# Changing when an attention kernel issues its loads, normalizations and PSUM copies

## The chip, the cores and the metric

The kernel runs on one core of a Trainium2 chip. The metric is device time in microseconds (us) of one execution. A core has five engines that run their own instruction streams: PE (TensorE, matrix products), ACT (ScalarE), DVE (VectorE), POOL (GpSimd) and SP (SyncE, which here only issues DMAs). An engine runs its instructions in the order in which they were put in its stream; a wait for a semaphore holds everything behind it on that engine. All data are float32.

## The reference

Two layers of attention over x of shape (4, 256, 64, 64), four images of 256 channels with 64 x 64 tokens each.

```python
# layer 0: 8 heads of 32 channels, 4096 queries, 1024 keys
n = GroupNorm32(x)
q = conv1x1(n, Wq); k = conv2x2_stride2(n, Wk); v = conv2x2_stride2(n, Wv)
a = softmax((q @ k + q @ (rel_h + rel_w)) * 32**-0.5)
x = x + a @ v
# layer 1: four areas of 1024 tokens per image, attention inside an area
n = GroupNorm32(x)
q, k, v = split(conv1x1(n, w_qkv) + b_qkv)          # 8 heads of 32
o = softmax(q @ k * 32**-0.5) @ v
x = x + conv1x1(o + depthwise7x7(v) + b_pe, w_proj) + b_proj
```

GroupNorm has no weights: each of 32 groups (8 channels by 4096 tokens) is brought to mean 0 and variance 1.

## The kernel before

**Blocks, units, steps, phases.** The work is cut into eight blocks: A0 to A3 and then B0 to B3 (`BLOCKS`), where A is layer 0 of an image and B is layer 1 of it. A block has 16 units (`UNITS`): eight chunks of 512 queries by two groups of four heads. A unit has eight steps (`NKT`): one tile of 128 keys each. So there are 128 units and 1024 steps. The main loop at the end of `direct_path` runs 683 phases (`PHASES`); a phase computes one full step and half a step (256 of the 512 queries), so 1.5 steps. A unit is thus 5 1/3 phases.

**What a phase does.** `scores` (L423) puts four heads' scores of its one and a half steps into three double PSUM banks; three exps on ACT (L465 twice, L476 for the half step) turn them into p in SBUF. Meanwhile PE multiplies the p of the phase before with v (`weighted`, L490), which adds up in a PSUM bank `av` for the whole unit. DVE adds up the same p into `acc` (`add_up`, L500), since a softmax needs the sum over all keys. Between these PE takes side work: one or two parts of a queue.

**End of a unit.** When a unit's last products with v are done, `evict` copies av to SBUF (`av_sb`, L1122, on ACT). There are two small PSUM banks in turn (`banks`): one holds av, the other serves side products (`ps_side`). When DVE's sums are complete, `divisors` (L509) adds them over partitions on PE, and `divide` copies the result (`den_sb`, L523, on ACT). Then it spreads the divisors over partitions by way of DRAM, all issued by POOL: `rows` (L524), `few` (L525), and later, after the reciprocal on DVE (L531), `recs` (L533) and four loads of `rb` (L535). The last step multiplies av_sb with rb into `att` (L538, DVE).

**What orders the rest.** Nothing reorders the program: each engine's stream is the order in which this Python code calls it. Four lists decide the order.

- `at(g, j, f)`: f is called at the end of the phase that reaches step j of unit g. Loads, means and variances, and hand-timed additions hang here. SP issues DMAs in the order of these calls.
- `task` and `task_at`: side work in parts (`side`), with a due time and a condition `ready`. `choose` takes the one with the earliest due time that is ready. `pressure` and `supply` reckon how many parts a phase must take; `credit` carries the rest over. Products of k, q, v, the value products, the projection and the convolution are such tasks, and each part is mostly one "side product" of 512 columns.
- `quick` (filled by `soon`): one entry at a time runs in a phase that has no other side work begun, no unit boundary and no division due. The group means and group variances of `plan_norm` (L347 to L364) go this way.
- `later`: normalizations on ACT (L387), run by `norm_next` at the end of a phase if the phase has room by `busy`, and if the phase number has reached `start`. If a task needs one that hasn't run, `settle` runs it at once. In the same way `normalize` runs the quick queue empty if its scale doesn't exist yet.

In the text a "call phase" is the phase of the loop in whose turn an instruction is put in the streams. Its DMA may issue later, if SP is held or behind.

**Normalizations.** `plan_norm` aggregates statistics at step j, and calls `means` at j + 1 and `variances` at j + 3. `variances` has one small product on PE, ACT's copy `gvar`, then three POOL operations: pow (L359), a product (L363) and a sign (L364), which give `norm_A` or `norm_B`. The normalizations read them: of `taps` (A's input for k and v, from `xa` loads), `hq` (A's chunk of queries, loaded by `fetch`, normalized 4 phases or more later), `h` (B's area, loaded by `load`, normalized at a planned step with no minimum), and `hv` (B's chunk for values, loaded at L950 by `plan_values`, 3 steps ahead of `when`, normalized 4 phases or more later).

**The convolution.** `plan_values` makes v for the whole image as `vout` and stores it to DRAM twice: to `vala` for the attention (L975) and, per column parity, to `vals` for the convolution (L983). The 7x7 depthwise convolution runs on PE as products with band matrices. A `share` is the data for 8 channels: a `band` of matrices (L1024) and rows of vals in `rows` or `share` tiles, by four DMAs. The first shares of an image are forced by `plan_conv`, `room` of them (2 for image 0, 3 for the others, which also use the space of weights no longer needed): each of these calls tests that less than `room` are loaded, then calls `load_share(True)`. `convolve` calls `load_share(False)` after each share that it has used. It stores its result as `cout` (L1055) to `conv`. `load_rest` loads it back as `cv` (L801, 16 row DMAs per chunk), `add_conv` (L813) adds it to att, and `project` (L828) ends with the output chunk. `load_v` (L739) loads `vc`, the attention's v, from vala.

**Buffers.** Chunk tiles (`xs`, `xa`, `hq`, `xc`, `hv`, `xm`, `cv`) share one pool of 6 buffers. `h` and the taps have 3, `vc` 4, `band` 2, `rows` 2, `vout` 2, `av_sb` 2, `rb` 1. A load into a buffer that is still in use waits on SP, and all later DMAs of SP with it.

Of the kernel before, what the change touches and what calls it, by code (L numbers as in the profile page):

```python
# [60 lines left out]
def direct_path(  # L61
# [124 lines left out]
    def at(g, j, f):  # L186
        g, j = g + int(j // NKT), int(j % NKT)
        plan.setdefault((g, j), []).append(f)
# [83 lines left out]
    def begun():  # L272
        return bool(side) and side[0][2]
# [57 lines left out]
    def plan_norm(key, g, j):  # L331

        name = f"{key[0]}{key[1]}"
        made = {}

        def aggregate():
            for tag, cols in (("mv", 2), ("gmean", 1), ("dev", 1), ("gvar", 1)):
                shape = [P, CT, cols] if cols > 1 else [P, CT]
                made[tag] = pool.tile(shape, FP, tag=tag, name=f"{tag}_{name}", bufs=2)
            mv = made["mv"]  # L340
            for t in range(CT):
                V.bn_aggr(out=mv[:, t, :], in_=stats[key][:, t].rearrange("p c s -> p (c s)"))

        def means():
            mv, mean, dev = made["mv"], made["gmean"], made["dev"]
            ps = ps_side(f"gm_{name}")[:, :CT]
            T.matmul(ps, lhsT=gmat, rhs=mv[:, :, 0], start=True, stop=True)  # L347
            S.copy(mean, ps)
            V.tensor_sub(dev, mv[:, :, 0], mean)
            V.tensor_mul(dev, dev, dev)  # L350
            V.tensor_add(dev, dev, mv[:, :, 1])

        def variances():
            ps = ps_side(f"gv_{name}")[:, :CT]
            T.matmul(ps, lhsT=gmat, rhs=made["dev"], start=True, stop=True)
            S.activation(made["gvar"], ps, AF.Identity, bias=eps)
            norm = pool.tile([P, 2, CT], FP, tag="norm", name=f"norm_{name}", bufs=8)
            shift, rstd = norm[:, 0, :], norm[:, 1, :]
            G.tensor_tensor(rstd, made["gvar"], neghalf, ALU.pow)  # L359
            if key == ("A", 0):  # L360
                V.scalar_tensor_tensor(shift, made["gmean"], -1.0, rstd, ALU.mult, ALU.mult)
            else:
                G.tensor_tensor(shift, made["gmean"], rstd, ALU.mult)  # L363
                G.tensor_scalar(shift, shift, -1.0, None, ALU.mult)  # L364
            norms[key] = shift, rstd

        def quietly(f, n):
            f()
            if key == ("A", 0):
                keep_busy(n)  # L370

        if key == ("A", 0):
            at(g - 1, 0, lambda: keep_busy(44))
        at(g, j, aggregate)
        at(g, j + 1, lambda: soon(lambda: quietly(means, 4)))
        at(g, j + 3, lambda: soon(lambda: quietly(variances, 10)))

    def normalize(key, dst, src, t, by_vector=False):
        while key not in norms:
# [169 lines left out]
    def plan_a(b, u, prep):  # L549
# [129 lines left out]
        for c in range(NCH):  # L679
            g = u + 2 * c  # L680
            at(g - 3, 4, lambda c=c: fetch(c))
            for t in range(CT):
                at(g - 2, 1 + 2 * t, lambda c=c, t=t: later(
                    ("hq", b, c), lambda: norm_chunk(c, t), fetched["q", c] + 4, True
                ))
            for qd in range(2):
                task_at(NKT * (g - 2) + 4, 2, make_q, c, qd, due=g - 0.3, ready=normed("hq", b, c))
            at(g + 3, 0, lambda c=c: load_residual(c))
            at(g + 4, 1, lambda c=c: add_residual(c))
            at(g + 4, 2, lambda c=c: store_chunk(c))  # L690
# [11 lines left out]

    def plan_b(b, u):
        key = ("B", b)
        hs = {}

        def load(a):
            hs[a] = pool.tile([P, CT, TA], FP, tag="h", name=f"h1_{b}_{a}", bufs=3)
            for half in range(2):
                nc.sync.dma_start(hs[a][:, :, half * CH : (half + 1) * CH], xmid[b][2 * a + half])  # L710
# [59 lines left out]
        for a in range(NAREA):  # L770
            g = u + 4 * a
            at(g - 6, 3, lambda a=a: load(a))
            for t in range(CT):
                at(g - 5, 2 + 3 * t, lambda a=a, t=t: later(("hs", b, a), lambda: norm(a, t), 0, True))
            for n in range(4):
                task_at(
                    NKT * (g - 4) + 1 + 4 * n, 2, make_k, a, n // 2, n % 2, due=g - 0.4, ready=normed("hs", b, a)
                )
            for n in range(4):
                at(g - 3, 1 + 2 * n, lambda a=a, n=n: load_v(a, n))  # L780
                at(g - 2, 1 + 2 * n, lambda a=a, n=n: make_v(a, n))
        for c in range(NCH):
            for qd in range(2):
# [77 lines left out]
        for c in range(NCH):  # L861
            g, j = (u + 2 * c + 4, 1) if b < B - 1 or c < NCH - 2 else (u + 2 * c + 3, 7)
            if b == B - 1 and c == NCH - 1:
                for t in range(CT):
                    at(g - 2, 2 + t, lambda c=c, t=t: load_rest(c, t))
                at(g - 2, 4, lambda c=c: load_residual(c))
                at(g - 1, 1, lambda c=c: add_conv(c, [0]))
                at(g - 1, 3, lambda c=c: project_last(c))
                continue
            for t in range(CT):  # L870
                at(g - 2, 7 + 4 * t, lambda c=c, t=t: load_rest(c, t))
            at(g - 1, 6, lambda c=c: load_residual(c))
            at(g, j, lambda c=c: add_conv(c))
            for to in range(CT):
                task_at(NKT * g + j + 2, 2, project, c, to, due=g + (2.2 if b < B - 1 else 3), lag=0)
# [67 lines left out]
    def plan_values(b, c, start):  # L943
# [44 lines left out]
                stored[b, c] = True  # L988

        when = int(start * NKT)  # L990
        at(0, when - 3, load)
        for t in range(CT):
            at(0, when + 5 + t, lambda t=t: later(("hv", b, c), lambda: norm(t), made["at"] + 4, True))
        for t in range(CT):
            task_at(
                when + 7, 2, values, t, due=start + 4,
# [6 lines left out]
    def load_share(must):  # L1003

        if not shares:
            return
        b, k = shares[0]
        for c in range(NCH):
            if must:
                need(stored, (b, c))  # L1010
            elif (b, c) not in stored:
                return
        shares.popleft()
        row, size = C * XT, TC * XT
        if b and (b * (C // TC) + k) % 3 == 2:
            place = const.tile([P, 2 * CT * 4 * C], FP, tag="wkv", name=f"share_{b}_{k}")
            n = 2 * NY * size
            xs = place[:NP, :n].rearrange("p (h y c x) -> p h y c x", h=2, y=NY, c=TC)
            band = place[:NP, n : n + 2 * TY * TX * TC].rearrange("p (h y m) -> p h y m", h=2, y=TY)
        else:  # L1020
            band = pool.tile([NP, 2, TY, TX * TC], FP, tag="band", name=f"band_{b}_{k}", bufs=2)
            xs = pool.tile([NP, 2, NY, TC, XT], FP, tag="rows", name=f"rows_{b}_{k}", bufs=2)
        loaded[b, k] = band, xs, phase[0]
        nc.sync.dma_start(band, mats[k])  # L1024
        for a in range(4):
            p = NP // 2 * (a % 2)
            nc.sync.dma_start(
                xs[p : p + NP // 2, a // 2].rearrange("p y c x -> p y (c x)")[:, :, : size - 3],
                bass.AP(
                    tensor=vals[b].tensor, offset=vals[b].offset + k * size + a,  # L1030
                    ap=[[row, NP // 2], [TY * TX * row, NY], [1, size - 3]],
                ),
            )
# [121 lines left out]
    while f < PHASES or before or plan or side or quick or norms_left or to_add or to_divide:  # L1155
# [12 lines left out]
        for s, u in before[:cut]:  # L1168
            accumulate(s, u)
        if cut:  # L1170
            evict(before[0][0] // NKT)
            copies[0] += 1
        exps[2]()
        _, rate = pressure()
        parts = done_den = 0
        if due and not begun():
            done_den = 1
            copies[0] += 1
            g = to_divide.popleft()
# [7 lines left out]
        elif quick and not begun() and not cut and f < PHASES:  # L1187
            quick.popleft()()
        else:
            wanted = credit + max(min(supply(), 2.0), min(rate, 2.0))  # L1190
            if rate > 2:
                parts = side_parts(4)
            elif rate > 1.5 or due or f >= PHASES or wanted >= (0.8 if cut else 1.5):
                parts = side_parts(2)
            elif begun() and side[0][0] % 2:
                parts = side_parts(1)
            elif boundary(mine):
                parts = side_parts(2) if wanted >= 0.9 else 0
            elif wanted >= 0.5 and not cut or begun():
                parts = side_parts(1)  # L1200
            credit = max(-0.5, min(wanted - parts, 0.5))
            if cut and not parts and not begun():
                banks.reverse()
        for s, u in before[cut:]:
            accumulate(s, u)
        add_ready()
# [617 lines left out]
```

## Time and profile before

| what | value |
|---|---|
| three runs | 3127.77, 3136.34, 3136.4 us; median 3136.34 |
| the profiled execution | 3135.3 us, span 3133.6 us |
| mean granted TensorE clock | 0.994 |
| PE | 3067.2 us busy, 98% |
| DVE | 2517.6 us, 80% |
| ACT | 2459.1 us, 78% |
| POOL | 485.4 us, 15% |
| instructions | 110020 |
| DMA | 423.71 MB, mean 135 GB/s |
| first exp begins | 71.2 us |
| last exp ends | 3107.5 us |

The span is from the first to the last recorded instruction; the profiled execution's own time is 1.7 us longer. The busy time of PE is modelled at its ends, so it says little about how close the loop is to its limit. The views used below are these. The page's fifth part lists groups of instructions: code line, engine, operation, destination and sources, shape and count, then busy time and mean duration in ns, then the idle time of that engine ahead of the group and what ended most of it. The waits of an engine list the waiting instruction, the producer it waited for, and after it total us, number and longest. The timeline has one line for each instruction or run of like instructions: start in us, duration, engine, code line, operation, tiles, count, and in brackets the wait ahead of it with what ended it. A queue such as SPq stands for the moment an engine issues a DMA. The windows view has one line for a stretch of time: its length, then for PE, PE's weight load, DVE, ACT and POOL the busy time with instruction counts, then the granted TensorE clock (PEclk), the mean busy share of the DMA engines, and GB/s.

### The profile page before, as it was taken

The numbers are of one execution on the slowest core, as the hardware profiler recorded it, in microseconds if no ns is written. First come the engines' busy times: TensorE is split into PE (matmuls) and PEld (weight loads), VectorE is DVE, ScalarE is ACT, GpSimd is POOL, SyncE is SP. The second block draws the span as 40 slices with busy tenths as digits, with TensorE's granted clock in tenths as the row PEclk, the third lists the DMA queues.
The fourth block names the chain that finished last, engine by engine and source line by source line (L and its number), as shares of the span: only waits on it lengthen the run. The fifth ranks groups of instructions, "written<-read, shape, count | busy, mean of one in ns | idle before, by whom it ended". The sixth has DMA issues, their size and how long they took to land. (4 is left out here: it accounts for less than half of the span.)

```text
span 3133.6 us, 110020 instructions
## 1 busy us (share of the span) xinstructions
PE 3067.2 (98%) x47254; PEld 1272.4 (41%) x47254; DVE 2517.6 (80%) x2721; ACT 2459.1 (78%) x2988; POOL 485.4 (15%) x921
## 2 busy tenths in 40 slices
PE   9999999999999999999999999999999999999998
PEld 6444443444344443334344443333444444343332
DVE  3788987788878778767688887777888888888888
ACT  3888887888888888778788787777777777787875
POOL 0111111112121111111112111111111111111111
PEclk9999999999999999999999999999999999999999
DMA  5344443565434566767865667767655555632222
GB/s 187 66 94 114 101 98 73 112 151 140 94 105 114 151 156 167 160 164 194 207 156 133 163 167 167 178 177 180 161 155 144 150 161 147 160 105 71 52 67 67
DMA packets 648323, 423.71 MB, mean 135 GB/s; under 512 B 411772, under 2 KB 556636, under 8 KB 647832
## 3 DMA queue, kind: packets, MB, share of 16 engines
q1 hardware_dynamic: 619384, 380.11, 47.9%
q0 software_dynamic: 28448, 36.48, 4.7%
q8 instruction: 379, 6.21, 0.9%
q14 instruction: 112, 0.92, 0.1%
HBM read 318.32 MB, written 98.09 MB: 133 GB/s over the span
## 5 line engine op out<-in xcount | busy, mean ns | idle before, releaser
L500 DVE TENSOR_TENSOR acc<-acc,p 128x1024 f32<-128x1024 f32 x1790 | 2113.6, 1218 | 436.9 <-PE av L490 190.5
L465 ACT ACTIVATE p<-s 128x1024 f32<-128x1024 f32 x1194 | 1160.0, 1024 | 432.8 <-PE s L423 417.6
L476 ACT ACTIVATE p<-s 128x1024 f32<-128x1024 f32 x598 | 617.9, 1033 | 0.7 <-PE ops L167 0.3
L423 PE MATMUL s<-q,k_A 32*64 32x256 f32 (+1 forms) x10928 | 555.6, 501 | 24.0 <-ACT p L465 21.7
L423 PE MATMUL s<-q,k_B 32*64 32x512 f32 (+1 forms) x10912 | 549.8, 497 | 4.4 <-ACT p L465 2.5
L490 PE MATMUL av<-p,v_A 128*32 128x256 f32 (+1 forms) x4784 | 454.0, 489 | 0.0
L490 PE MATMUL av<-p,v_B 128*32 128x512 f32 (+1 forms) x4776 | 451.3, 487 | 0.0
L423 PEld LDWEIGHTS s<-q,k_A 32*64 32x64 f32 x10928 | 260.4, 131 | 370.5 <-issue 140.7
L423 PEld LDWEIGHTS s<-q,k_B 32*64 32x64 f32 x10912 | 259.0, 130 | 348.5 <-issue 139.2
L535 POOL DMA_DIRECT2D rb<-recs x508 | 252.5, 503 | 548.8 <-DMA recs<-few 463.4
L533 POOL DMA_DIRECT2D recs<-few x127 | 70.1, 552 | 1401.1 <-DVE sums L532 1253.4
L490 PEld LDWEIGHTS av<-p,v_B 128*32 128x32 f32 x4776 | 149.8, 110 | 263.8 <-issue 237.7
L490 PEld LDWEIGHTS av<-p,v_A 128*32 128x32 f32 x4784 | 150.2, 110 | 230.8 <-issue 189.3
L465 ACT ACTIVATE acc<-s 128x1024 f32<-128x1024 f32 x172 | 166.9, 1023 | 86.4 <-PE s L423 86.4
L509 PE MATMUL den<-acc,ones 128*32 128x512 f32 x1024 | 142.7, 604 | 6.9 <-DVE acc L500 4.5
L525 POOL DMA_DIRECT2D few<-rows x127 | 71.4, 562 | 470.0 <-DMA rows<-den_sb 463.7
L167 PE MATMUL vals_ps<-hv,wqkv_sb 128*32 128x512 f32 x1024 | 126.7, 609 | 3.4 <-DVE xm L828 3.2
L167 PE MATMUL ops<-cv,wp_sb 128*32 128x512 f32 x1024 | 125.1, 598 | 4.9 <-DVE cv L813 2.9
L167 PE MATMUL k1ps<-h,wqkv_sb 128*32 128x512 f32 x1024 | 123.8, 598 | 2.6 <-ACT k_B L730 1.9
L167 PE MATMUL q1ps<-h,wqkv_sb 128*32 128x512 f32 x1024 | 124.5, 599 | 1.4 <-DVE xm L828 1.4
L167 PE MATMUL q0ps<-hq,wq_sb 128*32 128x512 f32 x1024 | 123.8, 597 | 1.2 <-ACT q L662 0.7
L167 PE MATMUL k0ps<-taps,wkv 128*32 128x256 f32 x2048 | 123.2, 382 | 0.4 <-ACT taps L387 0.4
(103 smaller groups left out, 2156.2 us busy)
## 6 DMA issues: line engine op xcount, KB each, us to landing
rows<-vals SPq DMA_DIRECT2D x384, 195.9 KB
rb<-recs POOLq DMA_DIRECT2D x508, 64.0 KB, 3.1
share<-vals SPq DMA_DIRECT2D x128, 195.9 KB
vala<-vout SPq DMA_DIRECT2D x128, 144.0 KB
vals<-vout SPq DMA_DIRECT2D x128, 144.0 KB
vc<-vala SPq DMA_DIRECT2D x64, 288.0 KB
band<-mats SPq DMA_DIRECT2D x96, 176.0 KB
hq<-in_x SPq DMA_DIRECT2D x32, 512.0 KB
```

The source lines that it names most:

```text
L167: T.matmul(out[cols, :], lhsT=lhsT[:, cols], rhs=rhs, start=start, stop=stop)
L423: T.matmul(out[n : n + WIDE], lhsT=unit[2]()[rows, unit[0], j * P + n : j * P + n + WIDE], rhs=unit[1]()[rows, cols], start=True, stop=True,)
L465: S.activation(p, (a, b)[n], AF.Exp, scale=SCALE)
L476: S.activation(p, c.rearrange("p b (l n) -> p b l n", l=2), AF.Exp, scale=SCALE)
L490: T.matmul(out, lhsT=v[:, j, unit[0] * P + HD * h : unit[0] * P + HD * h + HD], rhs=rhs, start=(j == 0 and not u), stop=(j == NKT - 1), sk ...
L500: V.tensor_add(to, to, p)
L509: T.matmul(dens[g][HD * h : HD * h + HD, :], lhsT=ones, rhs=p(h), start=(n == 0), stop=(n == len(sets) - 1),)
L525: G.dma_start(few[:, 0, :], rows.rearrange("h (q n) -> (h q) n", n=CH // HD))
L533: G.dma_start(recs.rearrange("h (q n) -> (h q) n", n=CH // HD), few[:, 1, :])
L535: G.dma_start(rb[HD * h : HD * h + HD, :], recs[h : h + 1, :].to_broadcast([HD, CH]))
```

## The change

It has five parts, all of which move calls to other phases; the arithmetic stays the same.

1. `plan_norm`: for all images but A0 (whose g is below 0) `variances` is queued at step j + 6 instead of j + 3.
2. Normalizations need older loads: hq at least 5 phases after its load (before 4), h at least 6 (before 0), hv at least 6 (before 4). To have it so, hv is loaded 5 steps ahead of `when` instead of 3.
3. `load_v` is called six steps sooner: at g - 4, step 3 + 2n, instead of g - 3, step 1 + 2n. `load_rest` is called at g - 2, steps 5 and 8, instead of 7 and 11.
4. `load_share(True)` does nothing if 3 shares (2 for image 0) are already loaded. Before, only the caller tested the number, against the room of its own image, while the share next in line can still belong to the image before.
5. In the loop, a phase that holds the end of a unit (`cut`) is called bare if it will take no side work and no division. In a bare phase `evict`'s copy of av comes behind the third exp on ACT; before, it was always ahead of the third exp. `wanted` is computed ahead of the exp for that, and `credit` is set from it.

```diff
-        at(g, j + 3, lambda: soon(lambda: quietly(variances, 10)))
+        at(g, j + (6 if g >= 0 else 3), lambda: soon(lambda: quietly(variances, 10)))
...
-                    ("hq", b, c), lambda: norm_chunk(c, t), fetched["q", c] + 4, True
+                    ("hq", b, c), lambda: norm_chunk(c, t), fetched["q", c] + 5, True
...
-        hs = {}
+        hs, since = {}, {}
 
         def load(a):
+            since[a] = phase[0]
...
-                at(g - 5, 2 + 3 * t, lambda a=a, t=t: later(("hs", b, a), lambda: norm(a, t), 0, True))
+                at(g - 5, 2 + 3 * t, lambda a=a, t=t: later(("hs", b, a), lambda: norm(a, t), since[a] + 6, True))
...
-                at(g - 3, 1 + 2 * n, lambda a=a, n=n: load_v(a, n))
+                at(g - 4, 3 + 2 * n, lambda a=a, n=n: load_v(a, n))
...
-                at(g - 2, 7 + 4 * t, lambda c=c, t=t: load_rest(c, t))
+                at(g - 2, 5 + 3 * t, lambda c=c, t=t: load_rest(c, t))
...
-        at(0, when - 3, load)
+        at(0, when - 5, load)
         for t in range(CT):
-            at(0, when + 5 + t, lambda t=t: later(("hv", b, c), lambda: norm(t), made["at"] + 4, True))
+            at(0, when + 5 + t, lambda t=t: later(("hv", b, c), lambda: norm(t), made["at"] + 6, True))
...
         b, k = shares[0]
+        if must and len(loaded) >= (3 if b else 2):
+            return
...
         if cut:
-            evict(before[0][0] // NKT)
             copies[0] += 1
-        exps[2]()
         _, rate = pressure()
         parts = done_den = 0
-        if due and not begun():
+        wanted = credit + max(min(supply(), 2.0), min(rate, 2.0))
+        bare = cut and not begun() and not due and f < PHASES and rate <= 1.5 and (wanted < 0.8 or not choose())
+        if cut and not bare:
+            evict(before[0][0] // NKT)
+        exps[2]()
+        if bare:
+            evict(before[0][0] // NKT)
+            banks.reverse()
+            credit = min(wanted, 0.5)
+        elif due and not begun():
...
-            wanted = credit + max(min(supply(), 2.0), min(rate, 2.0))
...
-            if cut and not parts and not begun():
-                banks.reverse()
```

## Prediction

> **What bounds the kernel now.** I read the page first, then the waits of ScalarE, then the timeline around the longest of them.
>
> ```profile
> PE 3067.2 (98%) x47254; PEld 1272.4 (41%) x47254; DVE 2517.6 (80%) x2721; ACT 2459.1 (78%) x2988; POOL 485.4 (15%) x921
> ...
> L465 ACT ACTIVATE p<-s 128x1024 f32<-128x1024 f32 x1194 | 1160.0, 1024 | 432.8 <-PE s L423 417.6
> ```
>
> TensorE (PE) looks full, but the share is no yardstick: its ends are modelled. So I measured the loop's own beat: from the timeline, the distance between the first L465 exp of one phase and of the next. Phases with one side product of 512 columns (four matmuls side by side) have a median of 3.794 us, with two 4.652 us. The difference, 0.858 us, is one such product, so these phases run at TensorE's pace of 2.937 + 0.857 x products; the second line agrees, for an exp that waits waits for PE's scores. Phases without side work take 3.25 us. By the program's order the 683 phases hold 1086 products and 38 have none: 645 x 2.937 + 1086 x 0.857 + 38 x 3.25 = 2948.6 us. First exp 71.2 us, after the last exp 26.1 us: 3045.9 of the span of 3133.6 us. The other 87.7 us are excess over the beat, four fifths of it in some 40 places. Only that can be won.
>
> ```profile
> ACT p L465 <- PE s L423: 417.6, 506, 2.9
> ...
> ACT hv L387 <- DMA hv<-xmid: 10.6, 3, 6.5
> ...
> ACT hq L387 <- DMA hq<-in_x: 7.4, 2, 6.6
> ACT hv L387 <- POOL norm_B L364: 6.1, 1, 6.1
> ```
>
> Columns are total us, times, longest. The first line is the beat. The other three are few and long: a normalization (L387) on ScalarE (ACT) waits for its load or its scale, all exps queue behind it, and PE runs dry. Three such events:
>
> ```profile
> 1346.86 0.39 SPq L1055 DMA_DIRECT2D conv<-cout  x1
> 1361.46 0.30 SPq L1024 DMA_DIRECT2D band<-mats  x1
> ```
>
> ```profile
> 1377.47 0.61 ACT L523 COPY den_sb<-den 128x512 f32<-128x512 f32 x1
> 1384.56 0.81 ACT L387 ACTIVATE hv<-hv,norm_B 128x512 f32<-128x512 f32 x1 [6.48 <-DMA hv<-xmid]
> ```
>
> At 1346.86 SyncE (SP) issued a store, and then nothing for 14.6 us: the next load, a band of convolution matrices, had to wait for its buffer. Everything behind it came late, an hv load too, and ACT stood 6.48 us.
>
> ```profile
> 1502.03 0.39 SPq L108 DMA_DIRECT2D hq<-in_x  x1
> ...
> 1510.43 0.81 ACT L387 ACTIVATE hq<-hq,norm_A 128x512 f32<-128x512 f32 x1 [6.57 <-DMA hq<-in_x]
> ...
> 1513.12 2.90 PE L423 MATMUL s<-q,k_A 32*64 32x256 f32 x28 [5.45 <-ACT p L465]
> ```
>
> Here hq was issued 22.7 us after its phase began (1479.3), and landed 8.4 us later: ACT waited 6.57 us, PE 5.45 us.
>
> ```profile
> 503.06 0.55 POOL L533 DMA_DIRECT2D recs<-few  x1 [11.27 <-DVE sums L532]
> 507.69 1.99 POOL L535 DMA_DIRECT2D rb<-recs  x4 [4.08 <-DMA recs<-few]
> 509.69 0.74 POOL L359 TENSOR_TENSOR norm_B<-gvar_B,neghalf 128x2 f32<-128x2 f32 x1
> ```
>
> The scale of the first hv (pow, L359) stood in GpSimd's (POOL's) queue behind rb, which waited for recs to land. ACT waited 6.13 us, and the phase took 6.76 us over its beat.
>
> ```profile
> 1380.00:1395.00 15.00, 8.82 (x108) 3.06 (x104) 9.00 (x11) 8.24 (x10) 3.12 (x6) 0.77 0.85 209
> ...
> 2200.00:2400.00 200.00, 200.00 (x3128) 82.28 (x3124) 166.18 (x171) 155.41 (x183) 32.56 (x63) 1.00 0.60 155
> ```
>
> In the third number from the end, PEclk, a stall shows a second time: 0.77 of 15 us, so 3.4 us of clock lost, against 1.00 in quiet stretches.
>
> **What the Trainium skill says.** "TensorE: Matmul & The Clock Gate", Part 1: the array falls to half rate after about one idle window of 3.4 us. The trace agrees: its clock records show 0.5 for 6.83 us from 511.4, 1258.9 and 1385.2, for 10.24 us from 1511.5 and for 3.41 us from 1931.3, each after such a stall. So a stall that goes takes up to 3.4 to 5.1 us of clock with it. "DMA: Bandwidth & Descriptors", Anatomy of one DMA: DMA engines do not wait on semaphores; the wait happens on the issuing sequencer before dispatch. The hole at 1346.86 agrees: what waits for a buffer holds all later DMAs of its queue. "Trainium Kernel Development and Optimization", Performance Expectations, calls matmul busy time a bad metric; 98% beside 87.7 us of excess agrees.
>
> **The change part by part**, from the order of both built programs and the durations above. Both hold 1086 products; phases without any go from 38 to 37, -0.3 us. The classes stay; what counts are stalls.
>
> *load_share.* Before, the first forced load for image 1 fetched image 0's share 30 as a third share, though two buffers exist; that is the hole (call phase 286, released by PE in 292). Now the guard returns, and share 30 is asked for in phase 291, when its buffer comes free. With hv loaded two steps (one to two phases) sooner as well, hv of phase 295 is issued some 25 us sooner than it was. What goes: phases 294-295 7.51 us over the beat, 297 1.34 (half clock), 299 and 301 0.91 (vout waiting for stores behind the hole), 305 2.52 (sums late because L958 waited 5.6 us for those stores). Together 12.3. I take 11, range 9 to 12.3. Its price: shares of image 1 are loaded two ahead, no longer three, so some are issued only 6 phases (28 us) before use. Cover is the 15 to 20 us that issue and landing take; if that is gone, PE waits at 317, up to 3 us.
>
> *Older loads.* By call phases, hq was normalized at least 4 phases after its load and is now at least 5, h 4 and now 6, hv 5 and now 6 or more. In phases 310 to 323 SP is never idle for long and lags its phases by 12 to 24 us (stores of vout took 2.5 to 4.4 us to issue); the excess is 1.56 + 2.33 + 9.54 - 0.32 = 13.1. hv in 310 and 318 (waits 1.67 and 2.45) now stands ahead of ten share DMAs and four stores, 7 to 12 us of issue: gone. But hq of 321 has the same place behind the same DMAs. If it still lands at 1510.4, its norm now ends phase 322 instead of 321: phase 324, at 1523.1 before, starts at 1511.2 + 4.65 = 1515.9, so 7.2 is won, or 3.9 if the clock still halves. I take 5, range 4 to 13.
>
> *Group means further apart.* Variances move 2 or 3 phases for images A2, A3, B2 and B3; for B0 and B1 they stay, since a normalization or the queue forces them, and so does the 6.76 at phase 102. Phase 158 (1.16 over) and 73 (0.67) are mended: 1.8. For A2 it costs: variances go from phase 73 to 76, and hq now leaves its place on ACT in 76 to the first taps of A2, which need that scale at once. Before, POOL and ACT did this there:
>
> ```profile
> 393.52 2.00 POOL L535 DMA_DIRECT2D rb<-recs  x4 [2.66 <-DMA recs<-few]
> 395.52 0.61 POOL L524 DMA_DIRECT2D rows<-den_sb  x1
> 398.76 0.58 POOL L525 DMA_DIRECT2D few<-rows  x1 [2.63 <-DMA rows<-den_sb]
> ```
>
> ```profile
> 393.80 0.60 ACT L523 COPY den_sb<-den 128x512 f32<-128x512 f32 x1
> 394.26 0.85 ACT L387 ACTIVATE hq<-hq,norm_A 128x512 f32<-128x512 f32 x1
> ```
>
> POOL's pow now comes behind rb, rows and few, and few waits for rows to land. So pow starts at 399.3; with L363 and L364 (1.96 us from 380.96 on, in phase 73) the scale is there at 401.3. ACT has copied den and gvar by 394.8 and waits 6.5 us; all exps of phase 77 wait behind it, as after 509.69. There 6.13 us of wait cost 6.76 + 1.20 (half clock): 8.0 us. I take 8 lost, range 5 (rows lands as fast as 1.7 us) to 9.
>
> *hv sooner* also asks for a chunk buffer sooner. One request cannot be met: hv 6 of image 1, in phase 254 instead of 256, needs a buffer that PE frees in phase 259.
>
> ```profile
> 1207.14 0.35 SPq L950 DMA_DIRECT2D hv<-xmid  x1
> ```
>
> Before, the ten share loads of phase 256 went out ahead, from 1192.95 to 1199.3. Now they stand behind this load, and go out from 1207.5 to 1214; PE wants them from 1218.5. At 5 to 8 us to land, PE waits 0 to 4. I take 1.5. The stores behind them come 7 us later and still end before 1228.9, when vout is wanted.
>
> *v and convolution results sooner.* 64 loads and 512 small ones are the same, earlier by 4 phases and by 1.3 to 2. DVE waited 1.69 for vc (2144) and 1.11 for cv; 461 and 463 are 2.51 over. Most DVE waits there are for rb (29.6 + 14.3 us), which these don't touch except by sharing queues. I take 2, range 0 (they collide with recs) to 5.
>
> *Copy behind the third exp.* In 9 bare phases av_sb (0.59 us) goes behind the exp that frees the last scores bank. Bare phases are 0.3 to 0.65 over and the one after up to 0.36. ACT's sum is the same, so only PE's earlier start counts: 2, range 0.5 to 4.
>
> Sum: 0.3 + 11 + 5 + 1.8 + 2 + 2 - 8 - 1.5 = 12.6 us. The profiled execution took 3135.3 us (span 3133.6 and 1.7 around it), 1 us under the median of 3136.34: 3122.7, say 3123.
>
> **Rivals.** (1) *The stalls go with their clock losses.* If hq lands under way (SP lagging 5 us less), older loads bring 9, load_share 12.3, DVE 4.5, copy 3, and rows lands fast (5 lost): 0.3 + 12.3 + 9 + 1.8 + 4.5 + 3 - 5 = 25.9, so 3109. For it: all min ages grow. Against: DMA share 0.75 to 0.85 there. (2) *Given back*: load_share 9, older loads 4, variances 0.7, copy 0.5, and 9 + 4 lost: about 3134. For it: SP and the DMA rings, not the age, set when things land around 1450 to 1510. (3) *Slower*: SP standing at hv 6 of image 1. If the share loads behind it take over 12 us to land instead of 8, PE stands over one window at 1219: 4 + 3.4 of clock, and vout at 1229 and 1233 waits 3.5 for its stores: 11 on top of rival 2, 3145. It decides from 4 us of wait on. Against: DMA share 0.61 there. (4) That the change doesn't do what it says is true for B0 and B1 and counted.
>
> **How the numbers follow.** Forecast 0.46 (3115 to 3129), rival 1 0.28, rival 2 0.14, rival 3 0.12. The range 3107 to 3136 leaves out the ends of rivals 1 and 3. About 0.3% (3126.9 to 3145.7) can't be told from no change; faster: 0.36 of the forecast, 0.28, 0.01: 0.65. Slower: 0.07 of rival 3. Same: 0.28.
>
> **What would show it.** No SP hole before band near 1347 and no hv wait at 1384; half-clock records from 1385 and perhaps 1511 gone; a new taps wait for norm_A of 5 to 7 us near 395 to 401, with a new half-clock record; norm_B's wait at 511 kept; an SP hole near 1181 to 1207; ACT's waits for hv and hq under 6 us together. It is wrong if taps don't wait near 401, or if excess grows in 345 to 470 (rb).

## The result and the profile after

The changed kernel takes 3111.24 us (median of four executions, 3109.85 to 3113.68). The kernel before, measured beside it, has a median of 3132.72 us over its four. The ratio is 0.9933, 95% interval 0.9914 to 0.9952, so the change made the kernel faster by 0.5 to 0.9%. The profiled execution took 3110.89 us, with a span of 3108.5 us.

The page's line of busy times and its line of the exps, of the changed kernel (columns as before):

```profile
PE 3059.6 (98%) x47254; PEld 1269.4 (41%) x47254; DVE 2517.8 (81%) x2721; ACT 2459.3 (79%) x2988; POOL 484.9 (16%) x921
...
L465 ACT ACTIVATE p<-s 128x1024 f32<-128x1024 f32 x1194 | 1161.4, 1026 | 428.1 <-PE s L423 416.7
```

Nothing was saved in work: the counts are the same, DVE and ACT are busy for the same time to 0.2 us. PE is busy for 7.6 us less with the same matmuls, which goes with the clock records further down. The exps wait for PE's scores as before (416.7 us for 417.6), so I take the beat as unchanged and look for the gain by place. I used the beat of the prediction again: a phase should take 2.937 us + 0.857 us for each side product, or 3.25 us with none. What a phase takes beyond that is its excess. Summed over stretches of phases, for two profiles of each kernel:

| phases | what lies there | before | before, again | after | after, again |
|---|---|---|---|---|---|
| 66-81 | scale of A2, first taps of A2 | 0.69 | 0.70 | 11.66 | 13.21 |
| 101-109 | scale of B0, first hv | 8.24 | 8.39 | 7.39 | 7.25 |
| 256-267 | hv 6 of image 1 | 1.99 | 1.99 | 3.41 | 3.25 |
| 268-281 | A3's vout and q | 9.33 | 8.77 | 5.95 | 7.47 |
| 282-293 | last shares of image 0 | 1.11 | 1.11 | 4.10 | 5.72 |
| 294-309 | behind the hole at 1346.86 | 12.60 | 10.67 | 1.40 | 1.45 |
| 310-323 | hq 7 of A3 (phase 321) | 13.65 | 12.47 | 2.11 | 2.54 |
| 412-471 | cv, vc, rb of B0 and B1 | 18.27 | 19.96 | 7.64 | 11.17 |
| others | | 21.9 | 21.7 | 15.8 | 15.2 |
| sum | | 87.7 | 85.8 | 59.5 | 67.3 |

Excess fell by 28.2 us in the first pair. The span fell by 25.1, because the first exp came at 74.4 us instead of 71.2 (the last section is on that). In the second pair, excess fell by 18.5 us. The first pair overstates the gain: the profiled execution of the kernel before took 3135.3 us, at the upper end of its executions (3127.77 to 3136.4), and the medians differ by 21.5 us. Stretches that differ between two profiles of one kernel (268 to 293 and 412 to 471 above all) say the least.

ScalarE's waits in the changed kernel (total us, times, longest us):

```profile
ACT taps L387 <- POOL norm_A L364: 6.5, 1, 6.5
...
ACT hv L387 <- POOL norm_B L364: 5.6, 1, 5.6
...
ACT hq L387 <- DMA hq<-in_x: 0.8, 1, 0.8
```

The first is new and was predicted at 6.5 us. The second is the old wait of phase 102, which was to stay. The long waits for hv and hq loads are gone: 0.8 us is left of the 18.0 before (10.6 and 7.4).

Where SP had stood for 14.6 us between a cout store and the next band (called the hole from here on), its issues now follow each other. Timeline of SP in the changed kernel (start, duration, queue, line, tiles, count):

```profile
1338.37 0.96 SPq L1058 DMA_DIRECT2D conv<-cout  x1
1339.43 0.41 SPq L1027 DMA_DIRECT2D band<-mats  x1
```

A new stall stands near 405 us. POOL and then ACT in the changed kernel (in brackets the wait ahead of the instruction):

```profile
396.83 1.99 POOL L535 DMA_DIRECT2D rb<-recs  x4 [2.69 <-DMA recs<-few]
398.81 0.59 POOL L524 DMA_DIRECT2D rows<-den_sb  x1
403.08 0.57 POOL L525 DMA_DIRECT2D few<-rows  x1 [3.68 <-DMA rows<-den_sb]
403.66 0.74 POOL L359 TENSOR_TENSOR norm_A<-gvar_A,neghalf 128x2 f32<-128x2 f32 x1
```

```profile
398.24 0.26 ACT L356 ACTIVATE gvar_A<-gv_A,eps 128x2 f32<-128x2 f32 x1 [0.47 <-PE gv_A L355]
405.03 0.61 ACT L387 ACTIVATE taps<-xa,norm_A 128x256 f32<-128x256 f32 x1 [6.53 <-POOL norm_A L364]
```

ACT had delivered gvar at 398.50. POOL could have used it from 399.40 on, but stood at few for rows to land, and the pow came at 403.66. All exps stood behind taps. The clock followed, as the windows view shows (third number from the end) for that stretch and for a quiet one:

```profile
400.00:415.00 15.00, 9.48 (x124) 3.90 (x122) 9.87 (x9) 8.13 (x10) 1.73 (x4) 0.77 0.56 112
2180.00:2380.00 200.00, 200.00 (x3124) 82.45 (x3120) 166.73 (x169) 155.09 (x181) 32.59 (x62) 1.00 0.60 157
```

The clock records at 0.5 inside the loop came to 34.1 us before (five records). Now there are two, 6.83 us from 405.7 and 3.41 us from 525.2 (four, with 17.1 us, in the second profile). At half rate that is up to 12 us of PE's time won back (half of 34.1 less half of 10.2, an estimate), if PE was what held the loop in them. It is part of the excess and not on top of it.

### The profile page after: what moved, and what is told of

Read it like the earlier page. It is cut to its first block, busy times and chain, and to the rows that moved or that the text cites. A ratio compares the mean times of both kernels' runs of the same rounds, so it can differ in the third digit from the quotient of the medians.

```text
span 3108.5 us, 110007 instructions
## 1 busy us (share of the span) xinstructions
PE 3059.6 (98%) x47254; PEld 1269.4 (41%) x47254; DVE 2517.8 (81%) x2721; ACT 2459.3 (79%) x2988; POOL 484.9 (16%) x921
## 5 line engine op out<-in xcount | busy, mean ns | idle before, releaser
L465 ACT ACTIVATE p<-s 128x1024 f32<-128x1024 f32 x1194 | 1161.4, 1026 | 428.1 <-PE s L423 416.7
L423 PE MATMUL s<-q,k_A 32*64 32x256 f32 (+1 forms) x10928 | 552.0, 499 | 15.8 <-ACT p L465 14.8
```

Of the source, the lines that this page charges most:

```text
L423: T.matmul(out[n : n + WIDE], lhsT=unit[2]()[rows, unit[0], j * P + n : j * P + n + WIDE], rhs=unit[1]()[rows, cols], start=True, stop=True,)
L465: S.activation(p, (a, b)[n], AF.Exp, scale=SCALE)
```

## The experiments

Two theories stood after the result. The first is the prediction's: each part mends its own stalls, the guard in `load_share` those of phases 294 to 309, the older loads those of 310 to 323. The rival: the backlog of SP behind one hole made both, and the guard alone mends both. The older loads and the later variances were not tried alone on the kernel before, nor was the guard taken out of the changed kernel. The older loads were taken out of the changed kernel instead, and the later variances for two of the images.

Ratios are to the kernel before on the same chip, with 95% intervals; excess is reckoned as above, from one profile of each. The changed kernel itself was run beside only two of the others, `hq`'s age alone and the last one; all others are compared with it through their ratios.

### The two kernels once more

> The kernel before once more, unchanged, for a second profile: executions of it lay between 3118 and 3136 us, and the first profile is at the upper end (3135.3). If the stalls in question belong to the program, phases 294 to 309 show 10 to 12.6 us over the beat again, 310 to 323 9 to 13.6, 101 to 109 about 8.2, and the spread lies in 268 to 281 (4.6 to 9.3 so far) and 412 to 471 (14 to 18). If they were chance of that one execution, the first two stretches fall below 5.

> The changed kernel once more, on the same chip as the next two: 3108 to 3114 us, with 11 to 12 us over the beat in phases 66 to 81, 1 to 2 in 294 to 309, 1 to 3 in 310 to 323, 6 to 8 in 412 to 471. A second profile tells what of it is chance.

The kernel before took 3133.64 us in this one execution. Its excess is in the table: 294 to 309 and 310 to 323 came again with 10.7 and 12.5 us. The stalls belong to the program. The changed kernel took 3113.32 us (median of six), ratio 0.9937 (0.9918 to 0.9956); 66 to 81 was a little above what I expected (13.2), and 412 to 471 too (11.2). So differences of 2 to 4 us in 412 to 471 between single profiles say nothing.

### The guard alone

```diff
         b, k = shares[0]
+        if must and len(loaded) >= (3 if b else 2):
+            return
```

> The kernel before with only the guard in load_share. Theory (the third share's load into a full pool was the hole in SP's stream, and everything behind it came late): the excess over the beat in phases 294 to 309, 12.6 us before, falls to 1 to 4 us, no half-clock record near 1385, while phases 282 to 293 may rise by up to 3 us (as in the changed kernel); elsewhere as before. About 8 us less than before, ratio 0.9975. Rival (hv was late because it was issued too late, and the hole only coincides): the hv wait of phase 295 stays above 4 us and the stretch above 9 us; ratio 0.999 to 1.000.

3110.81 us against 3126.79, ratio 0.9947 (0.9932 to 0.9963): 16.0 us, twice the gain of my theory. Phases 294 to 309 fell to 0.67 us, without the record near 1385; hv no longer waited there, though its load is called in the same phase, 290. But phases 310 to 323, where I expected nothing, fell from 13.65 to 0.75 us. The two falls sum to more than the 16.0 us, partly since that profile of the kernel before is from the upper end; in the three other profiles with the hole these stretches have 10.4 to 10.8 and 9.3 to 12.5 us. SP and ACT in this kernel:

```profile
1484.17 0.39 SPq L108 DMA_DIRECT2D hq<-in_x  x1
```

```profile
ACT hq L387 <- DMA hq<-in_x: 1.8, 2, 1.3
```

The same hq load, with the same minimum age of 4 phases, was issued 15.0 us after the start of its call phase instead of 22.7, and ACT waited 0.49 us for it instead of 6.57. Of all SP issues in call phases 292 to 299, the median lag was 19.7 us before and 7.7 us with the guard; in 310 to 316, 19.2 and 11.9. Phase by phase, the median lags of the two kernels differ by 14.7 us in call phase 289, by 7.7 us at this hq, and by 0.4 us in 323. So half of the hole was still there 150 us after it, though PE's stalls in between gave SP time to catch up. The rival holds, as far as this kernel goes: with the guard, hq's lag is just short enough.

### Sooner loads of v and of convolution results, alone and taken out

```diff
-                at(g - 3, 1 + 2 * n, lambda a=a, n=n: load_v(a, n))
+                at(g - 4, 3 + 2 * n, lambda a=a, n=n: load_v(a, n))
...
-                at(g - 2, 7 + 4 * t, lambda c=c, t=t: load_rest(c, t))
+                at(g - 2, 5 + 3 * t, lambda c=c, t=t: load_rest(c, t))
```

> The kernel before with only load_v and load_rest sooner. Theory (in the layer-1 blocks the small cv loads went out together with the divisor DMAs; apart from them rb lands in time, and PE no longer waits for DVE's xm): phases 412 to 471, 18.3 us over the beat before, fall to about 8 us as in the changed kernel (7.7), att_B's waits for rb fall from 29.6 to about 16 us, the half-clock record at 1931 goes; about 10 us less than before, ratio 0.997. Rival (that stretch was mended by the older loads or by the shifted phases of SP, not by these loads): 412 to 471 stay above 15 us, att_B's waits above 25 us, ratio 0.999 to 1.000.

3121.25 us, ratio 0.9981 (0.9974 to 0.9987). Phases 412 to 471 fell to 6.4 us, att_B's waits for rb to 17.6 us, and the record at 1931 is gone, as the theory had it. The median fell by 5.5 us, half of what I expected and of what the two profiles show in this stretch (11.9).

> The changed kernel with load_v and load_rest where they were. Theory (the sooner loads keep the divisors' DMAs clear of the cv bursts, whatever the other parts do): phases 412 to 471, 7.7 us over the beat in the changed kernel, rise to 14 to 17 us, att_B's waits for rb from 15.8 to 25 us or more; ratio to before 0.995 to 0.997. Rival (with the guard's earlier SP stream the bursts no longer collide): 412 to 471 stay below 10 us, ratio 0.993.

3117.38 us, ratio 0.9974 (0.9964 to 0.9984), which is clear of the changed kernel's 0.9933 and 0.9937; the stretch rose to 16.0 us, but att_B's waits for rb only to 20.2, not to 25. Over all profiles, the nine with the sooner loads have 6.3 to 11.3 us there, the five with the old ones 14.2 to 20.0. Phases 461 and 463 tell best, together 2.1 to 3.0 us in each of the five and less than 0.1 in the nine. DVE's waits for DMAs in 300 us around there, first of the changed kernel, then without the sooner loads:

```profile
DVE att_B L538 <- DMA rb<-recs: 5.2, 3, 3.1
```

```profile
DVE att_B L538 <- DMA rb<-recs: 11.9, 6, 3.1
...
DVE cv L814 <- DMA cv<-conv: 3.1, 1, 3.1
DVE v_B L747 <- DMA vc<-vala: 1.4, 1, 1.4
DVE few L531 <- DMA few<-rows: 1.2, 1, 1.2
```

With the old loads, cv, vc and rb all come late to DVE; xm comes late behind them, and PE stands for a bank that xm frees (1.5 and 1.3 us in these 300 us, and not at all in the changed kernel). That rb alone is the reason, as I expected, is not so: over the whole run att_B's waits for rb are 23.2 us without the bare copy and 27.5 us with the younger hq (two kernels further down), both with sooner loads, and 412 to 471 stay at 11.3 and 9.0 there. v's transpose waits for vc once, for 1.4 to 2.0 us and ahead of phase 461, in each of the five profiles with the old loads and in none of the nine, so 461 and 463 point to `load_v`. Which of the two loads brings the rest wasn't tried.

### The copy behind the third exp, alone and taken out

The diff is the one of the loop in the section on the change.

> The kernel before with only the copy of av behind the third exp in bare phases. Theory (PE gets the last scores bank 0.6 us sooner): bare phases fall from 0.26 us over the beat on average to about 0.1, the phases after them from 0.49 to 0.24, together 4 to 5 us; no stall elsewhere moves by more than 1 us except by chance of DMA timing; ratio 0.9985. Rival (the copy behind the exp makes PE's next unit wait for the av bank just as long): the sum over these 24 phases stays within 1 us of the 9.0 before, ratio 1.000.

3122.51 us, ratio 0.9990 (0.9982 to 0.9997). The order on ACT differs in nine phases, not in the twelve that I had counted. Each with the phase behind it, they have 7.55 us of excess before, and 7.55 in each of the three other profiles without the change. Here they have 3.78. So the copy brings 3.8 us. All of it comes in the phases behind (4.8 us before, 1.1 now). The bare phases themselves, which I had expected to fall too, stay at 2.7 us. The profile's other gains lie in stretches that vary between profiles, and the medians differ by 4.3 us.

> The changed kernel with the copy of av always ahead of the third exp. Theory: bare phases and those behind them go from 4.3 us over the beat back to about 9; the 2.2 us of phases 67 to 69 (k_A's two additions and the statistics come together on DVE there) go, since they come from side work that bare phases' credit moved; in all 2 to 4 us slower than the changed kernel, ratio to before 0.994 to 0.995. Rival (the copy is worth nothing): within 1 us of the changed kernel, 0.993.

3115.74 us, ratio 0.9964 (0.9950 to 0.9977). The nine bare phases of this program, with those behind them, go from 3.21 to 7.55 us. The 2.2 us of phases 67 to 69, which I put down to bare phases, stayed (3.8 here, as in the second profile of the changed kernel). By its ratio this kernel is some 8 to 10 us slower than the changed kernel, with intervals that just overlap, and not 2 to 4. Its other stretches are much as in that second profile, so the rest isn't explained.

### The older loads taken out

```diff
-                    ("hq", b, c), lambda: norm_chunk(c, t), fetched["q", c] + 5, True
+                    ("hq", b, c), lambda: norm_chunk(c, t), fetched["q", c] + 4, True
...
-                at(g - 5, 2 + 3 * t, lambda a=a, t=t: later(("hs", b, a), lambda: norm(a, t), since[a] + 6, True))
+                at(g - 5, 2 + 3 * t, lambda a=a, t=t: later(("hs", b, a), lambda: norm(a, t), 0, True))
...
-        at(0, when - 5, load)
+        at(0, when - 3, load)
...
-            at(0, when + 5 + t, lambda t=t: later(("hv", b, c), lambda: norm(t), made["at"] + 6, True))
+            at(0, when + 5 + t, lambda t=t: later(("hv", b, c), lambda: norm(t), made["at"] + 4, True))
```

> The changed kernel with the normalizations' minimum ages and the hv load as before (hq 4 phases, h 0, hv 4, hv loaded three steps ahead). Theory (the waits of 310 to 323 came from SP's backlog behind the hole, which the guard removes; the ages had no part in it): phases 310 to 323 stay at 1 to 3 us over the beat, no wait of ACT for hq or hv above 1.5 us, SP's hole at hv 6 of image 1 is gone and phases 256 to 267 fall from 3.4 to 2.0; in all 0 to 2 us faster than the changed kernel, ratio to before 0.992 to 0.995. Rival (the prediction's step: the ages carry these 5 us or more): hq or hv waits of 2 us or more come back in 310 to 323, the stretch is above 7 us; ratio 0.995 to 0.997.

3101.3 us, ratio 0.9917 (0.9903 to 0.9931), with 50.1 us of excess, 9 to 17 less than the two profiles of the changed kernel. In time the interval overlaps that of the changed kernel (0.9914 to 0.9952), so the gain shows by place and not clearly in the total. Phases 256 to 267 went back to 1.98 us and 282 to 293 to 1.44. Phases 310 to 323 stayed at 2.7 us, but with one wait for hq of 2.8 us, so neither side of my expectation holds cleanly. The surprise is phases 66 to 81: 1.19 us instead of 11.66. Here the variances of A2 are later too, and POOL's order is as bad:

```profile
400.53 0.57 POOL L525 DMA_DIRECT2D few<-rows  x1 [2.40 <-DMA rows<-den_sb]
401.11 1.13 POOL L359 TENSOR_TENSOR norm_A<-gvar_A,neghalf 128x2 f32<-128x2 f32 x1
402.33 0.52 POOL L363 TENSOR_TENSOR norm_A<-gmean_A,norm_A 128x2 f32<-128x2 f32 x1
...
402.94 1.19 POOL L364 TENSOR_SCALAR norm_A<-norm_A 128x2 f32<-128x2 f32 x1
```

```profile
406.61 1.16 ACT L387 ACTIVATE taps<-xa,norm_A 128x256 f32<-128x256 f32 x2
```

The scale is there at 404.13, and the first taps come at 406.61 without a wait. An hq of the old age took its place on ACT in phase 76, so taps came in phase 79, three phases later than in the changed kernel.

### hq's age alone, and A2's variances alone

```diff
-                    ("hq", b, c), lambda: norm_chunk(c, t), fetched["q", c] + 5, True
+                    ("hq", b, c), lambda: norm_chunk(c, t), fetched["q", c] + 4, True
```

> The changed kernel with hq's minimum age alone back at 4 phases. Theory (the stall of phase 76 takes two parts together: the later variances and the older hq, which yields its place on ACT to the first taps; with hq in its place the variances run in phase 77 and taps first need them in 79): phases 66 to 81 fall from 11.7 to 1 to 1.5 us over the beat, no half-clock record near 406, and 310 to 323 stay at 1 to 4; 9 to 11 us less than the changed kernel. Rival (the variances alone bring it, whatever hq does): the stretch stays above 8 us, and the time within 2 us of the changed kernel.

3109.66 us, ratio 0.9929 (0.9910 to 0.9949), 3.7 us under the changed kernel beside it, not 9 to 11. The stall went as expected: 66 to 81 fell to 1.18 us. But 310 to 323 rose to 8.26, beyond what I allowed. The timeline of this kernel at that place:

```profile
1486.08 0.39 SPq L108 DMA_DIRECT2D hq<-in_x  x1
...
1495.23 0.81 ACT L387 ACTIVATE hq<-hq,norm_A 128x512 f32<-128x512 f32 x1 [7.25 <-DMA hq<-in_x]
...
1497.92 2.90 PE L423 MATMUL s<-q,k_A 32*64 32x256 f32 x32 [6.13 <-ACT p L465]
```

So the wait of hq was back, with the guard in place.

```diff
-        at(g, j + (6 if g >= 0 else 3), lambda: soon(lambda: quietly(variances, 10)))
+        at(g, j + (6 if g >= 0 and key != ("A", 2) else 3), lambda: soon(lambda: quietly(variances, 10)))
```

> The changed kernel with variances of image A2 alone back at step j + 3. Theory (A2's scale came behind rows and few on POOL, taps waited 6.53 us for it, and the clock halved for 6.8 us): phases 66 to 81 fall from 11.7 us over the beat to about 1 as before, no half-clock record near 405; the rest as in the changed kernel, 3100 us, ratio to before 0.990. Rival (the scale is only the last of several things late there, taps' loads or the sums would wait instead): the stretch stays above 6 us; 3106 to 3110 us.

3103.56 us, ratio 0.9925 (0.9911 to 0.9939), which again overlaps with the changed kernel's interval. Phases 66 to 81 fell to 2.60 us and no clock record is near 405. So the stall takes both parts: later variances with an hq of the old age, or early variances with the older hq, don't have it. The 2.2 us of phases 67 to 69 stayed, where DVE adds the position terms to k_A next to statistics and sums. They are absent from all three kernels with later variances and the old age of hq (the third is the last one below), so they come with the older hq; that it is by side work that it moved is my reading.

### What decides hq of phase 321

The last load of hq of A3 (call phase 317) stands with different neighbours in the fourteen profiles. Lag is from the start of call phase 317 to SP's issue.

| kernel | lag, us | normalized in phase | ACT waited, us | excess of 310-323 |
|---|---|---|---|---|
| before | 22.7 | 321 | 6.57 | 13.65 |
| before, again | 21.2 | 321 | 6.84 | 12.47 |
| sooner v and cv alone | 21.2 | 321 | 7.68 | 9.25 |
| copy alone | 19.9 | 321 | 5.74 | 10.25 |
| after, hq's age 4 | 20.4 | 321 | 7.25 | 8.26 |
| last kernel below | 18.9 | 321 | 4.52 | 8.02 |
| after, no older loads | 17.3 | 321 | 2.76 | 2.68 |
| guard alone | 15.0 | 321 | 0.49 | 0.75 |
| after | 11.3 | 322 | 0 | 2.11 |
| after, again | 11.0 | 322 | 0 | 2.54 |
| after, v and cv loads as before | 11.1 | 322 | 0 | 1.41 |
| after, copy always ahead | 10.8 | 322 | 0 | 3.11 |
| after, A2 near | 10.2 | 322 | 0 | 0.70 |
| last but one kernel below | 10.1 | 322 | 0 | 1.65 |

Wherever ACT waited, the normalization began 7.9 to 9.3 us after the issue. So with hq in 321 the lag decides: from about 15 us on, ACT stands. The guard takes the lag of the hole away, but not always enough: in the four kernels with the guard and hq in 321, the median lag in call phases 292 to 299 is 5.7 to 7.7 us, and yet hq's lag is 15.0, 17.3, 18.9 and 20.4. By phases 310 to 316 the median is 11.9 to 15.6 us again, without any hole; what sets this second lag wasn't tried. An hq of age 5 works in two ways: it is normalized in 322, and side work moves so that a vout's four stores (call phase 314, issued from 1467.3 to 1471.5 us in the kernel with hq's age 4, and with the next load at 1473.6) go out in phase 322, behind hq instead of ahead of it. In these kernels the normalization began 14.9 to 16.0 us after the issue. Against the 7.9 to 9.3 us above that is 6 to 8 us later than it could, by my estimate.

### Two versions with the new stall mended

```diff
-        at(g, j + (6 if g >= 0 else 3), lambda: soon(lambda: quietly(variances, 10)))
+        at(g, j + (6 if g >= 0 and key not in (("A", 2), ("B", 0)) else 3), lambda: soon(lambda: quietly(variances, 10)))
...
-            plan_values(b, c, (18.4, 43, 52, 72)[b] + (1.7, 0.9, 1.4, 1.7)[b] * c)
+            plan_values(b, c, (19.2, 43, 52, 72)[b] + (1.7, 0.9, 1.4, 1.7)[b] * c)
```

> The changed kernel with variances of images A2 and B0 at step j + 3, and image 0's values planned to begin 0.8 units later (19.2 for 18.4), so that norm_B of B0 goes to POOL ahead of rb's wait and hv needs it four phases later. Theory: phases 66 to 81 at 2.6 us as with A2 alone, phases 101 to 109 fall from 7.4 to below 1 us, no half-clock record between 390 and 530; 17 to 18 us less than the changed kernel, 3092 to 3096, ratio 0.9885 to 0.990. Rival (values that start later crowd the convolution or another normalization waits in turn): one stall of 3 us or more appears between phases 103 and 300; 3099 to 3105.

3097.73 us, ratio 0.9909 (0.9894 to 0.9923), just outside what I expected. Phases 101 to 109 fell to 2.0 us, not below 1; the wait for norm_B and the clock records between 390 and 530 are gone. POOL in this kernel, with the scale ahead of rb's wait instead of behind it:

```profile
502.13 1.19 POOL L364 TENSOR_SCALAR norm_B<-norm_B 128x2 f32<-128x2 f32 x1
504.84 0.63 POOL L533 DMA_DIRECT2D recs<-few  x1 [1.51 <-DVE sums L532]
507.15 2.01 POOL L535 DMA_DIRECT2D rb<-recs  x4 [1.67 <-DMA recs<-few]
```

The first hv came at 519.47 without a wait. Excess is 42.9 us. The last kernel has the same edits on the changed kernel without the older loads:

> The changed kernel without the older loads (ages and hv load as before), with variances of A2 and B0 at step j + 3 and image 0's values from 19.2 units on. If the stretches add up as the single runs show: 66 to 81 about 0.7, 101 to 109 about 2, 256 to 267 2.0, 282 to 293 1.4, the rest as without the older loads: 39 to 42 us over the beat, 3090 to 3095 us, 17 to 20 us less than the changed kernel. If another normalization gets late instead (younger hq with SP behind): one new wait of ACT of 3 us or more, and 3097 or above.

3099.67 us, ratio 0.9900 (0.9880 to 0.9919), 13.7 us under the changed kernel on its chip. It has 50.6 us of excess, not 39 to 42, mostly because hq of 321 waited 4.52 us again and the clock halved for 10.24 us from 1486.8 (310 to 323: 8.0 us). All its executions are below all of the changed kernel beside it. The one before it has only its ratio, whose interval overlaps the changed kernel's a little. The two were not measured beside each other, so which is faster is open.

## Why the prediction was right, and where it was not

The time (3111.24 us) lies in the range, on the side that was forecast. It lies near the 3109 us of rival 1, 12 us under the forecast; part of that nearness is luck, as the end of this section says. By its steps, with excess before minus after in the first pair of profiles:

- *The beat and the places of stalls.* Right. Beside the later first exp, nothing but excess changed.
- *load_share*, 11 us (9 to 12.3). Right for its own stretch: 11.2 us in 294 to 309, and 11.9 with the guard alone. The price feared at phase 317 didn't come.
- *Older loads*, 5 us (4 to 13). The stretch gave 11.5 us, inside the range, but the step was argued wrongly. The text said that hq "has the same place behind the same DMAs" and took its landing at 1510.4 as given. It didn't ask why SP lagged by 22.7 us there. 7.7 us of that lag were left from the hole, and the guard alone, with hq at its old age, gives 12.9 us. Nor has the older hq the same place: four stores go behind it, and with the guard its lag is 10.1 to 11.3 us instead of 15.0 to 20.4. So it is a second, independent cover: with it the stretch stays at 0.7 to 3.1 us in all profiles, without it at 0.75 to 8.3 once the guard is in. Taken back alone, hq's age is worth 5.7 us there (2.54 to 8.26), but 0.6 when the other ages and the hv load go back with it (2.11 to 2.68). On their own account the older loads cost 1.4 us in 256 to 267, and A2's stall needs the older hq. Phases 282 to 293 rose by 3.0, but they have 1.4 and 3.3 us in two kernels without the older loads, so that cost isn't shown.
- *Group means*, 8 lost and 1.8 won. The mechanism and the wait (6.53 us for 6.5) were right, down to hq leaving its place. The cost was mis-sized: 7.33 us in phase 76 and 1.48 in 78 are 8.8, and 2.2 in 67 to 69, from moved side work, were not seen: 11.0 in the stretch. The 1.8 us of phases 158 and 73 came to 1.0 (1.16 to 0.40 and 0.67 to 0.41). The cost was also put under one head: later variances without the older hq cost little there (1.18 and 1.19 us in two kernels with hq's old age, 0.69 before); it takes both parts. A1's variances stay as well, since its g is below 0 like A0's.
- *hv sooner*, 1.5 us lost. Right: 1.4 us, which is what PE waited for rows there. SP issued hq at 1188.96 and then hv only at 1215.84, when PE freed the buffer; the ten share loads went out behind it.
- *v and convolution results*, 2 us (0 to 5). Mis-sized: 10.6 us in the first pair, 8.8 in the second, 11.9 alone, and 8.4 when taken out (4.9 against the second profile); in medians 5.5 alone. The text said that these loads don't touch most of DVE's waits "except by sharing queues". That exception carries the larger part, as far as it is known. Phase 416 (4.9 us in one profile, 1.5 in the other) is DVE's lateness, and varies.
- *Copy*, 2 us (0.5 to 4). The mechanism was right and the size too small: 3.8 us alone, and 4.3 when taken out. The text read the phases behind the bare ones as up to 0.36 us over; four of the nine have 0.88, and that is where the gain lies.
- *Rivals.* Rival 3, SP standing at hv 6 for so long that the clock halves, didn't decide: phase 262, which waited for rows, was 1.67 us over its beat, and no clock record follows it. Rival 2 named SP's lag as what sets landing times, which is true; but it took the lag of 1450 to 1510 as there to stay.

Rival 1's terms came closest because it had SP lag 5 us less. Its A2 stall (5) was too low by 6.0 us and its DVE term (4.5) by 6.1. That the two cancel is luck. The forecast's own miss of 12 us is mostly 8.6 us for v and the convolution results and 6.5 for 310 to 323, less 3.0 for A2.

## What to carry to other kernels

When a queue that works in order stands, ask how long its backlog lives, not only what waits first: compare the issue lag of its transfers phase by phase, with the hole and without it, and charge to the hole only the lag that goes with it. Here that was 7.7 us of 22.7. A stall that needs two edits together shows only when each is taken out of the sum, so test by removal as well as by addition. If a normalization is made later, look at what takes its place on the engine, and whether that has its own inputs yet.

## What was not expected of the hardware

The same instructions up to the first exp took 71.2 to 75.4 us. The clock records tell the executions apart: with none at 0.5 near the start, the first exp came at 71.2 and 71.4 us (two profiles); with one of 3.41 us between 16 and 20 us, at 72.3 to 73.9 us (seven); with one of 6.83 us, at 72.7 to 75.4 us (five). The last two ranges overlap, so the records don't tell all of it, and no run tested the cause. Two profiles of one kernel differ by 1.1 us (before) and 1.6 us (after) there, the fourteen by 4.2. So a comparison of single profiles should be made from the first exp on.
